# Keys and values of a cross-attention context by seven block products in place of eight

## The chip, the cores and the metric

The kernel runs on one core of a Trainium2 chip. The metric is the device time of one launch in microseconds (us). The engines are called as in the profile: PE (matrix products; PEld is its weight load), DVE (vector), ACT (scalar), POOL (GpSimd) and SP (it only issues DMA transfers here). Each engine takes its instructions strictly in the order in which the program lists them, and waits on semaphores for the others.

## The reference

One transformer block in float32: 16 batch elements of 224 tokens with 512 features, a context of 750 tokens with 512 features for each, 16 heads of 32 features. Biases are left out here:

```python
x_norm = modulate(_ln(x), shift_a, scale_a)            # shift, scale, gate from cond
x = x + gate_a[:, None] * (attention(x_norm) @ W_proj)
q_c  = _ln(x) @ W_qc
kv_c = _ln(context) @ W_kvc                            # (16, 750, 512) @ (512, 1024)
k_c, v_c = jnp.split(kv_c, 2, axis=-1)
x = x + softmax(q_c k_c^T * scale) v_c @ W_cproj       # 16 heads
h = gelu(modulate(_ln(x), shift_m, scale_m) @ W_mlp1) @ W_mlp2
x = x + gate_m[:, None] * h
```

The change touches the lines of `kv_c`, and the residual `x` of the cross attention.

## The kernel before

Three stages follow each other: self attention (to about 728 us), cross attention (about 728 to 2192 us) and the MLP. The change lies in the cross attention, and the MLP already computes its products by blocks in the Winograd form of Strassen's method: seven products of half-sized blocks in place of eight, with sums of blocks made by `combine` and `combine_right`.

**Layout.** A unit is one batch element `b` and one group `g` of four heads (128 features). There are 16 x 4 = 64 units. The context of 750 tokens is six chunks `c` of 125 (`CP`, `CC`), or two halves `hf` of 375 (`HS`). `turn_ctx` transposes a normalised context chunk on PE into PSUM, and ACT copies it into `cxt` (features on partitions). `project_k(b, m, hf)` makes 128 features of the keys for one half by four matmuls of 375 columns, evicted by ACT into `kt`. `project_v(b, c)` makes all 512 features of the values of a chunk by four matmuls of 512 columns, evicted by ACT into `vt`. For each batch element that is 32 matmuls of 375 and 24 of 512. A float32 matmul of the program shows as two records in the trace.

**PSUM.** Eight banks: `ps_s` is one tile of four banks (`sc`, the scores of two context chunks for four heads), `ps_mm` has three banks (`mm`, for projections, transposes and the transposed maxima), `ps_o` one (`o`).

**A unit in three rounds.** `Unit` is a software pipeline over three units: `cur` computes scores, `prev` exponentials, `last` values. The loop is

```python
if last:
    last.values()                       # PE: o <- pt,vt and o <- acc,ones (the "sums")
for n in range(CH):                     # CH = 3
    st = cur.scores(n)                  # PE into sc
    if n == 0 and last:
        last.finish()                   # DVE: reciprocal, product
    cur.keep(n, st)                     # DVE: running maximum "top" (2 ops); ACT: copy pt <- sc
    run(plan, (b, g, 2 * n))            # slot 2n: other work, planned by hand
    if n < 2 and prev:
        prev.subtract(n)                # PE: o <- mc; DVE: pt <- pt,o (3 ops)
    if n == 0 and prev:
        prev.weights(0)                 # ACT: 3 exponentials; POOL: 5 sums "acc"
    run(plan, (b, g, 2 * n + 1))        # slot 2n+1
    if n == 1 and prev:
        prev.weights(1)
cur.maxima()                            # PE transposes of top; DVE: mc
```

The table `plan` holds the other work by (batch element, unit, slot), filled by `at_slot`: six slots in each unit. In it lie the projections of keys and queries for the next unit, the values and transposes of the next batch element, the layer norms (`Norm`: statistics on DVE, the rest on POOL), the loads, and `project` (the attention's output product with the residual) of the batch element before. In `project` DVE adds the bias to the product (`upd<-mm,bcproj`), POOL adds that to `x`, and a store to `x_cross` follows when both chunks of 112 tokens are done. `Ordered` keeps every engine in the order of the calls, so the slot decides the place on every queue.

Of the kernel before, what the change touches and what calls it, by code (L numbers as in the profile page):

```python
# [37 lines left out]
def kernel(  # L38
# [112 lines left out]
    def load_x(pool, src, bufs):  # L151
        t = pool.tile([TP, TC, H], F32, name="x", bufs=bufs)
        nc.sync.dma_start(out=t, in_=src)
        return t
# [232 lines left out]
    def run(plan, key):  # L387
        for f in plan.pop(key, ()):
            f()
# [371 lines left out]
    def gelu(ps, h, m):  # L761
        nc.scalar.activation(h, ps, AF.Gelu_apprx_tanh, bias=bcol[:, o_mlp + m : o_mlp + m + 1])

    class First:


# [62 lines left out]


    wqc, wcproj, wkc, wvc = cw["qc"], cw["proj"], cw["k"], cw["v"]
    cxt_pool = context_pools.enter_context(tc.tile_pool(name="cxt", bufs=3, side="right", reuse_waits="tile"))
    with tc.tile_pool(name="ca", bufs=2, reuse_waits="tile") as ca:
        xs = {}
        xns = {}
        cxt = {}
        xt = {}
        qt = {}
        kt = {}
        vt = {}  # L840
        at = {}
        norms = {}

        def turn_ctx(b, c):
            if c % CH == 0:
                cxt[b, c // CH] = cxt_pool.tile([P, KC, HS], F32, name="cxt")
            ps = ps_mm.tile([P, 512], F32, name="mm")
            for k in range(KC):
                turn(ps[:, k * CP : (k + 1) * CP], cx[b, c][:, k * P : (k + 1) * P], ident[:CP, :CP])
            lo = (c % CH) * CP  # L850
            nc.scalar.copy(
                cxt[b, c // CH][:, :, lo : lo + CP], ps[:, : KC * CP].rearrange("p (k t) -> p k t", k=KC)
            )

        def project_k(b, m, hf):
            if hf == 0:
                kt[b, m] = ca.tile([P, S], F32, name="kt", bufs=2)
            ps = ps_mm.tile([P, 512], F32, name="mm")
            for k in range(KC):
                mm(  # L860
                    ps[:, :HS], wkc[:, k, m * P : (m + 1) * P], cxt[b, hf][:, k, :],
                    start=(k == 0), stop=(k == KC - 1),
                )
            nc.scalar.activation(
                kt[b, m][:, hf * HS : (hf + 1) * HS], ps[:, :HS], AF.Identity,
                bias=bcol[:, o_kvc + m : o_kvc + m + 1],
            )

        def project_v(b, c):
            vt[b, c] = ca.tile([CP, H], F32, name="vt", bufs=2 * CC)  # L870
            ps = ps_mm.tile([P, 512], F32, name="mm")
            lo = (c % CH) * CP
            for k in range(KC):
                mm(
                    ps[:CP, :H], cxt[b, c // CH][:, k, lo : lo + CP], wvc[:, k, :],
                    start=(k == 0), stop=(k == KC - 1),
                )
            nc.scalar.copy(vt[b, c], ps[:CP, :H])

        def fetch(b):  # L880
            xs[b] = load_x(ca, x_self[b], 3)

        def norm_begin(b):
            xns[b] = ca.tile([TP, TC, H], F32, name="xn", bufs=1)
            norms[b] = Norm(
                [xns[b][:, c, :] for c in range(TC)], [xs[b][:, c, :] for c in range(TC)], TP
            )

        def turn_x(b, k):
            if k == 0:  # L890
# [19 lines left out]

        def project(b, c, ps=None):
            if ps is None:
                ps = ps_mm.tile([P, 512], F32, name="mm")
            whole(project_heads(ps, at[b], wcproj, c * TP))
            add_to_x(ca, ps[:TP, :H], xs[b][:, c, :], bcproj[0], None)
            if c == TC - 1:
                lo = b % GB * N
                nc.sync.dma_start(
                    out=x_cross[b // GB][lo : lo + N, :].rearrange("(c p) d -> p c d", p=TP), in_=xs[b]
                )  # L920

        bcproj = []

# [5 lines left out]
        def at_slot(b, g, slot, f):  # L929
            plan.setdefault((b, g, slot), []).append(f)  # L930

        for b in range(B):
            n = b + 1
            for g in range(KC):
                f, m = (b, g + 1) if g < KC - 1 else (n, 0)
                if f < B:
                    for hf in range(2):
                        at_slot(b, g, hf, lambda f=f, m=m, hf=hf: project_k(f, m, hf))
                    at_slot(b, g, (5, 3, 5, 5)[g], lambda f=f, m=m: project_q(f, m))
            if b:  # L940
                at_slot(b, 1, 4, lambda b=b: project(b - 1, 0))
                at_slot(b, 3, 4, lambda b=b: project(b - 1, 1))
            else:
                for c in range(4):
                    at_slot(0, c // 2, 3 + c % 2, lambda c=c: project_v(0, c))
                at_slot(0, 2, 0, make_bcproj)
            at_slot(b, 0, 2, lambda b=b: project_v(b, 4))
            at_slot(b, 0, 4, lambda b=b: project_v(b, 5))
            if n < B:

                for c in range(CH):
                    at_slot(b, 0, 3 if b else 5, lambda n=n, c=c: turn_ctx(n, c))
                    at_slot(b, 2, 3, lambda n=n, c=c: turn_ctx(n, CH + c))
                for c, (u, slot) in enumerate(((1, 2), (2, 2), (2, 4), (3, 3))):
                    at_slot(b, u, slot, lambda n=n, c=c: project_v(n, c))
                for k in range(0, KC, 2):
                    at_slot(b, 3, 2, lambda n=n, k=k: turn_x(n, k))
                at_slot(b, 0, 0, lambda n=n: fetch(n))
                at_slot(b, 1, 1, lambda n=n: norm_begin(n))
                at_slot(b, 1, 1, lambda n=n: norms[n].stats(0))  # L960
                at_slot(b, 1, 3, lambda n=n: norms[n].stats(1))
                at_slot(b, 2, 0, lambda n=n: norms[n].apply())
            if n == B:


                for c in range(4):
                    at_slot(b, 0, 1 + c, lambda c=c: mlp_load(c))
                    at_slot(b, 1, 1 + c, lambda c=c: mlp_norm(c))
                at_slot(b, 2, 2, mlp_begin)
                at_slot(b, 3, 1, lambda: mlp_weights(cw["pool"], "wqc"))  # L970
                for c, (u, slot) in enumerate(((2, 4), (2, 5), (3, 1), (3, 2))):
                    at_slot(b, u, slot, lambda c=c: mlp_turn(ps_mm, c))
            if b + 2 < B:
                for hf in range(2):
                    at_slot(b, 2 * hf, 3 if b or hf else 5, lambda b=b, hf=hf: load_ctx(b + 2, hf))
                    for c in range(CH):
                        at_slot(
                            b, 1 + 2 * hf, (4, 5, 5)[c] - hf, lambda b=b, hf=hf, c=c: cnorms[b + 2, hf].stats(c)
                        )
                    at_slot(b + hf, 3 - 3 * hf, 0, lambda b=b, hf=hf: cnorms[b + 2, hf].apply())  # L980
        for hf in range(2):
            for c in range(CH):
                at_slot(0, hf, 1 + hf + c // 2, lambda hf=hf, c=c: cnorms[1, hf].stats(c))
            at_slot(0, hf, 2 + hf, lambda hf=hf: cnorms[1, hf].apply())

        class Unit:

# [108 lines left out]
            def finish(self):  # L1096
                t = ca.tile([P, N], F32, name="at", bufs=2 * KC)
                normalize(ca, self.o, t)
                at.setdefault(self.b, []).append(t)

        fetch(0)
        for hf in range(2):
            for c in range(hf * CH, (hf + 1) * CH):
                turn_ctx(0, c)
            load_ctx(1, hf)
            project_k(0, 0, hf)
        for k in range(0, KC, 2):
            turn_x(0, k)
        project_q(0, 0)

        units = [(b, g) for b in range(B) for g in range(KC)]
        cur = prev = last = None
        for b, g in units:
            cur, prev, last = Unit(b, g), cur, prev
            if last:
                last.values()
            for n in range(CH):
                st = cur.scores(n)
                if n == 0 and last:
                    last.finish()  # L1120
                cur.keep(n, st)
                run(plan, (b, g, 2 * n))
                if n < 2 and prev:
                    prev.subtract(n)
                if n == 0 and prev:
                    prev.weights(0)
                run(plan, (b, g, 2 * n + 1))
                if n == 1 and prev:
                    prev.weights(1)
            cur.maxima()  # L1130
# [212 lines left out]
```

## Time and profile before

| | |
|---|---|
| median of three runs | 2908.67 us (2907.1 to 2912.02) |
| profiled execution: its span | 2906.1 us; no other time is known of it |
| PE busy | 2834.6 us, 98% |
| DVE, ACT, POOL busy | 1926.2, 1119.7, 1201.5 us |
| granted TensorE clock, mean | 0.993 |
| keys, `mm<-cxt,wkvc` of 375 | 1024 records, 355.0 us |
| values, `mm<-wkvc,cxt` of 512 | 768 records, 354.4 us |
| one batch element in the steady part of the cross attention | 90 us |

The profiled execution's time is its span, from its first instruction to its last. It lies 2.6 us below the median of the runs. "Busy" is time in which an engine had an instruction; a small share of the span is no measure of whether that engine makes others wait. Times of instructions are from the start of the span. In a timeline, the bracket behind a row tells how long the engine stood idle before it, and which work ended that.

### The profile page before, as it was taken

The numbers are of one execution on the slowest core, as the hardware profiler recorded it, in microseconds if no ns is written. First come the engines' busy times: TensorE is split into PE (matmuls) and PEld (weight loads), VectorE is DVE, ScalarE is ACT, GpSimd is POOL, SyncE is SP. The second block draws the span as 40 slices with busy tenths as digits, with TensorE's granted clock in tenths as the row PEclk, the third lists the DMA queues.
The fourth block names the chain that finished last, engine by engine and source line by source line (L and its number), as shares of the span: only waits on it lengthen the run. The fifth ranks groups of instructions, "written<-read, shape, count | busy, mean of one in ns | idle before, by whom it ended". The sixth has DMA issues, their size and how long they took to land. (4 is left out here: it accounts for less than half of the span.)

```text
span 2906.1 us, 47040 instructions
## 1 busy us (share of the span) xinstructions
PE 2834.6 (98%) x19733; PEld 1810.3 (62%) x19733; DVE 1926.2 (66%) x2764; ACT 1119.7 (39%) x1402; POOL 1201.5 (41%) x1357
## 2 busy tenths in 40 slices
PE   8999999998999999999999999999979999999999
PEld 3444444444555565555656556556546888888888
DVE  4666776676478778787787787877775643444343
ACT  1222222221356655665566556655643112112211
POOL 1022222122356666676666766666551210221021
PEclk9999999998999999999999999999999999999999
DMA  5111110100100010100101100000013111110110
GB/s 191 59 33 33 32 33 10 60 11 24 57 32 24 23 35 24 35 26 21 35 24 35 35 19 28 27 33 24 22 44 107 55 37 37 44 58 29 45 44 30
DMA packets 55384, 114.43 MB, mean 39 GB/s; under 512 B 4308, under 2 KB 4372, under 8 KB 55172
## 3 DMA queue, kind: packets, MB, share of 16 engines
q1 hardware_dynamic: 54560, 110.58, 11.8%
q8 instruction: 155, 2.54, 0.4%
q10 hardware_dynamic: 612, 0.85, 0.1%
q14 instruction: 57, 0.47, 0.1%
HBM read 89.33 MB, written 22.09 MB: 38 GB/s over the span
## 5 line engine op out<-in xcount | busy, mean ns | idle before, releaser
L28 POOL TENSOR_TENSOR acc<-acc,pt 125x448 f32<-125x448 f32 x504 | 573.6, 1138 | 39.5
L28 ACT COPY pt<-sc 125x1792 f32<-125x1792 f32 x192 | 317.3, 1653 | 563.1 <-DVE top L28 510.1
L28 DVE TENSOR_TENSOR pt<-pt,o 125x896 f32<-125x896 f32 x384 | 394.2, 1081 | 88.1 <-PE o L28 85.5
L28 DVE TENSOR_TENSOR top<-top,sc 125x896 f32<-125x896 f32 x320 | 346.4, 1083 | 35.4 <-PE sc L28 28.7
L28 PE MATMUL mm<-wkvc,cxt 128*125 128x512 f32 x768 | 354.4, 604 | 6.9 <-ACT kt L28 6.9
L28 PE MATMUL mm<-cxt,wkvc 128*128 128x375 f32 x1024 | 355.0, 489 | 2.3 <-ACT cxt L28 2.3
L28 ACT ACTIVATE pt<-pt 125x896 f32<-125x896 f32 x384 | 338.4, 951 | 20.0 <-DVE pt L28 19.4
L28 POOL TENSOR_TENSOR upd<-upd,gate 112x512 f32<-112x512 f32 (+1 forms) x60 | 79.2, 1321 | 632.9 <-DVE upd L28 628.4
L28 POOL TENSOR_TENSOR acc<-pt 125x448 f32<-125x448 f32 x126 | 143.8, 1141 | 447.7 <-ACT pt L28 447.7
L28 PEld LDWEIGHTS mm<-cxt,wkvc 128*128 128x128 f32 x1024 | 185.6, 191 | 119.8 <-issue 16.6
L28 DVE RECIPROCAL at<-o 128x224 f32<-128x224 f32 x128 | 198.6, 1552 | 72.9 <-PE o L28 72.9
L28 PEld LDWEIGHTS mm<-wkvc,cxt 128*125 128x125 f32 x768 | 136.5, 187 | 171.5 <-issue 153.2
L28 ACT ACTIVATE pt<-sc 112x1792 f32<-112x1792 f32 x64 | 106.5, 1663 | 333.8 <-PE sc L28 333.8
L28 POOL TENSOR_TENSOR rstd<-mv,eps 112x2 f32<-112x2 f32 (+3 forms) x93 | 18.0, 193 | 508.8 <-DVE mv L28 508.8
L28 PE MATMUL sc<-qt,kt 32*125 32x224 f32 x3072 | 201.6, 377 | 14.0 <-ACT pt L28 13.4
L28 PE MATMUL mm<-xt,wqkv 128*128 128x448 f32 x512 | 208.6, 550 | 5.7 <-DVE xt L28 4.7
L28 DVE TENSOR_REDUCE m<-sc 112x8 f32<-112x1792 f32 x64 | 129.6, 2025 | 121.8 <-PE sc L28 121.8
L28 PEld LDWEIGHTS sc<-qt,kt 32*125 32x125 f32 x3072 | 133.1, 183 | 94.1 <-issue 33.8
L28 PE MATMUL o<-pt,vt 125*32 125x224 f32 x3072 | 158.6, 354 | 0.0
L28 PEld LDWEIGHTS mm<-xt,wqkv 128*128 128x128 f32 x512 | 92.0, 190 | 87.6 <-issue 80.4
L28 DVE TENSOR_REDUCE mc<-mm 112x8 f32<-112x512 f32 (+1 forms) x128 | 79.8, 665 | 98.3 <-PE mm L28 98.3
L28 ACT COPY mx<-a 128x512 f32<-128x512 f32 x26 | 15.2, 586 | 327.0 <-POOL upd L28 307.9
(185 smaller groups left out, 4656.5 us busy)
## 6 DMA issues: line engine op xcount, KB each, us to landing
cx<-in_ctx_dram SPq DMA_DIRECT2D x96, 250.0 KB
x<-in_x_dram SPq DMA_DIRECT2D x16, 448.0 KB
x_self<-x SPq DMA_DIRECT2D x16, 448.0 KB
x<-x_self SPq DMA_DIRECT2D x16, 448.0 KB
x_cross<-x SPq DMA_DIRECT2D x16, 448.0 KB
mx<-x_cross SPq DMA_DIRECT2D x28, 256.0 KB
w<-in_L_xcond_W_mlp_dram SPq DMA_DIRECT2D x7, 1024.0 KB
xr<-x_cross SPq DMA_DIRECT2D x28, 256.0 KB
```

The source lines that it names most:

```text
L28: return lambda *args, **kw: self.tc.keep_in_program_order(f(*args, **kw))
```

## The change

Keys and values are computed by blocks. For the keys the two halves of W's columns, the two halves of the features and the two halves of the context's tokens make 2 x 2 blocks. `kv_sums` makes the three sums of blocks of the weights once on DVE (four operations each for keys and values); `ctx_sums` makes the sums of blocks of each context on POOL (four operations of 128 x 750). `project_k(b, r)` makes 128 features of each of two groups `r` and `r + 2`, for all 750 tokens, by seven products of two matmuls of 375 columns; `project_v(b, c)` makes chunks `c` and `c + 3` by seven products of two matmuls of 256 columns. The products run by a generator, `seven`, in four steps that the plan lays in four slots. Two products stay in PSUM and are added to:

```python
def seven(product, bank, keep, add):      # keep: ACT evicts; add: DVE adds PSUM to what was kept
    a = bank()
    product(a, 1, True)
    keep((0, 0), a)
    c = bank()
    product(c, 2, True)
    add((0, 0), c)
    yield
    product(a, 6, False)
    keep((0, 1), a)
    yield
    b = bank()
    product(b, 5, True)
    keep((1, 1), b)
    product(a, 7, False)
    add((1, 1), a)
    yield
    product(b, 3, False)
    add((0, 1), b)
    product(a, 4, False)
    keep((1, 0), a)
```

For each batch element that is 28 matmuls of 375 and 42 of 256. Four products of seven are evicted by ACT and three added by DVE. The plan is laid anew (`u` is the unit's place; the groups come in the order 0, 2, 1, 3):

```diff
+            steps(b, ((0, 0), (0, 1), (0, 3), (0, 4)), lambda b=b: project_k(b, 1))
+            steps(b, ((1, 0), (1, 1), (1, 1), (1, 2)), lambda b=b: project_v(b, 1))
+            steps(b, ((1, 2), (1, 3), (1, 3), (1, 4)), lambda b=b: project_v(b, 2))
             if b:
-                at_slot(b, 1, 4, lambda b=b: project(b - 1, 0))
-                at_slot(b, 3, 4, lambda b=b: project(b - 1, 1))
+                for c in range(TC):
+                    at_slot(b, 0, 1 + c, lambda b=b, c=c: fetch_rest(b - 1, c))
+                    at_slot(b, 1, 1 + 2 * c, lambda b=b, c=c: bias_rest(b - 1, c))
+                    at_slot(b, 2, 1 + 2 * c, lambda b=b, c=c: project(b - 1, c))
...
-                for c in range(CH):
-                    at_slot(b, 0, 3 if b else 5, lambda n=n, c=c: turn_ctx(n, c))
-                    at_slot(b, 2, 3, lambda n=n, c=c: turn_ctx(n, CH + c))
...
+                for c in range(CC):
+                    at_slot(b, 2, c // CH * 2, lambda n=n, c=c: turn_ctx(n, c))
+                at_slot(b, 2, 2, lambda n=n: ctx_sums(n))
+                for k in range(0, KC, 2):
+                    at_slot(b, 2, 4, lambda n=n, k=k: turn_x(n, k))
+                steps(b, ((3, 0), (3, 1), (3, 2), (3, 3)), lambda n=n: project_k(n, 0))
+                steps(b, ((3, 3), (3, 4), (3, 4), (3, 5)), lambda n=n: project_v(n, 0))
...
+                    at_slot(b, 2, 3, lambda b=b, hf=hf: load_ctx(b + 2, hf))
...
+                            b + hf, 3 - 3 * hf, 1 + c, lambda b=b, hf=hf, c=c: cnorms[b + 2, hf].stats(c)
```

So all six transposes of a context, its sums, and both chunks of `project` fall into the third unit of a batch element (before: transposes and `project` each in two units).

The residual is no longer kept from its load to `project`: `fetch` normalises the loaded tile in place, and `fetch_rest` loads each chunk of 112 tokens again later. POOL adds the bias to it (`bias_rest`), DVE adds the product, and each chunk is stored by itself:

```diff
-            add_to_x(ca, ps[:TP, :H], xs[b][:, c, :], bcproj[0], None)
-            if c == TC - 1:
-                lo = b % GB * N
-                nc.sync.dma_start(
-                    out=x_cross[b // GB][lo : lo + N, :].rearrange("(c p) d -> p c d", p=TP), in_=xs[b]
-                )
+            t = xr.pop((b, c))
+            nc.vector.tensor_tensor(t, ps[:TP, :H], t, ALU.add)
+            lo = b % GB * N + c * TP
+            nc.sync.dma_start(out=x_cross[b // GB][lo : lo + TP, :], in_=t)
```

More of the change, by code (lines that the diff above doesn't have):

```diff
@@ L762, in gelu @@
         nc.scalar.activation(h, ps, AF.Gelu_apprx_tanh, bias=bcol[:, o_mlp + m : o_mlp + m + 1])
+    def seven(product, bank, keep, add):
[5 more added lines that the diff above has]
+        add((0, 0), c)
+        yield
+        product(a, 6, False)
+        keep((0, 1), a)
+        yield
+        b = bank()
[3 more added lines that the diff above has]
+        add((1, 1), a)
+        yield
+        product(b, 3, False)
+        add((0, 1), b)
+        product(a, 4, False)
+        keep((1, 0), a)
     class First:
@@ L831, with kv_sums @@
     wqc, wcproj, wkc, wvc = cw["qc"], cw["proj"], cw["k"], cw["v"]
-    cxt_pool = context_pools.enter_context(tc.tile_pool(name="cxt", bufs=3, side="right", reuse_waits="tile"))
+    cxt_pool = context_pools.enter_context(tc.tile_pool(name="cxt", bufs=2, side="right", reuse_waits="tile"))
+    lo2, hi2 = slice(0, 2), slice(2, 4)
+    wlo, whi = slice(0, HT), slice(HT, H)
+    def kv_sums(w, name):
+        ws = cxt_pool.tile([P, 3, 2, HT], F32, name=name, bufs=1)
+        every(combine(
+            nc.vector, w[:, lo2, wlo], w[:, hi2, wlo], w[:, lo2, whi], w[:, hi2, whi],
+            ws[:, 0], ws[:, 1], w[:, lo2, whi], ws[:, 2],
+        ))
+        return {
+            1: w[:, lo2, wlo], 2: w[:, hi2, wlo], 3: ws[:, 2], 4: w[:, hi2, whi],
+            5: ws[:, 0], 6: ws[:, 1], 7: w[:, lo2, whi],
+        }
     with tc.tile_pool(name="ca", bufs=2, reuse_waits="tile") as ca:
-        xs = {}
+        xr = {}
         xns = {}
         cxt = {}
+        cxb = {}
         xt = {}
@@ L842, with mm_bank @@
         norms = {}
+        kv_blocks = []
+        order = (0, 2, 1, 3)
+        def mm_bank():
+            return ps_mm.tile([P, 512], F32, name="mm")
         def turn_ctx(b, c):
@@ L846, in turn_ctx @@
                 cxt[b, c // CH] = cxt_pool.tile([P, KC, HS], F32, name="cxt")
-            ps = ps_mm.tile([P, 512], F32, name="mm")
+            ps = mm_bank()
             for k in range(KC):
@@ L853, in turn_ctx @@
             )
[L855 to L862, printed above, removed]
-                )
[L864 to L867, printed above, removed]
@@ L869, in project_v @@
-        def project_v(b, c):
[L870 to L878, printed above, removed]
-        def fetch(b):
-            xs[b] = load_x(ca, x_self[b], 3)
@@ L883, in norm_begin, with ctx_sums @@
[L883 to L887, printed above, removed]
+        def ctx_sums(b):
+            x0, x1 = cxt[b, 0], cxt[b, 1]
+            tt = cxt_pool.tile([P, 3, 2, HS], F32, name="ctt", bufs=1)
+            every(combine_right(
+                nc.gpsimd, x0[:, lo2], x1[:, lo2], x0[:, hi2], x1[:, hi2],
+                tt[:, 0], tt[:, 1], x1[:, lo2], tt[:, 2],
+            ))
+            cxb[b] = {
+                1: x0[:, lo2], 2: x0[:, hi2], 3: x1[:, hi2], 4: tt[:, 2],
+                5: tt[:, 0], 6: tt[:, 1], 7: x1[:, lo2],
+            }
@@ new lines, in project_k, with product, place, keep @@
+        def project_k(b, r):
+            for i in range(2):
+                kt[b, r + 2 * i] = ca.tile([P, S], F32, name="kt", bufs=4)
+            def product(ps, p, begin):
+                for k in range(2):
+                    mm(
+                        ps[:, :HS], kv_blocks[0][p][:, k, r * P : (r + 1) * P], cxb[b][p][:, k, :],
+                        start=(begin and k == 0), stop=(k == 1), skip_group_check=True,
+                    )
+            def place(at):
+                return kt[b, r + 2 * at[0]][:, at[1] * HS : (at[1] + 1) * HS]
+            def keep(at, ps):
+                m = o_kvc + r + 2 * at[0]
+                nc.scalar.activation(place(at), ps[:, :HS], AF.Identity, bias=bcol[:, m : m + 1])
+            def add(at, ps):
+                nc.vector.tensor_tensor(place(at), ps[:, :HS], place(at), ALU.add)
+            return seven(product, mm_bank, keep, add)
@@ new lines, in project_v, with product, place, keep @@
+        def project_v(b, c):
+            for i in range(2):
+                vt[b, c + CH * i] = ca.tile([CP, H], F32, name="vt", bufs=10)
+            def product(ps, p, begin):
+                for k in range(2):
+                    mm(
+                        ps[:CP, :HT], cxb[b][p][:, k, c * CP : (c + 1) * CP], kv_blocks[1][p][:, k, :],
+                        start=(begin and k == 0), stop=(k == 1), skip_group_check=True,
+                    )
+            def place(at):
+                return vt[b, c + CH * at[1]][:, at[0] * HT : (at[0] + 1) * HT]
+            def keep(at, ps):
+                nc.scalar.copy(place(at), ps[:CP, :HT])
+            def add(at, ps):
+                nc.vector.tensor_tensor(place(at), ps[:CP, :HT], place(at), ALU.add)
+            return seven(product, mm_bank, keep, add)
@@ new lines, in fetch, with fetch_rest, bias_rest @@
+        def fetch(b):
+            xns[b] = t = ca.tile([TP, TC, H], F32, name="xn", bufs=1)
+            nc.sync.dma_start(out=t, in_=x_self[b])
+            ts = [t[:, c, :] for c in range(TC)]
+            norms[b] = Norm(ts, ts, TP)
+        def fetch_rest(b, c):
+            xr[b, c] = t = ca.tile([TP, H], F32, name="xr", bufs=3)
+            nc.sync.dma_start(out=t, in_=x_self[b][:, c, :])
+        def bias_rest(b, c):
+            nc.gpsimd.tensor_tensor(xr[b, c], xr[b, c], bcproj[0], ALU.add)
@@ L912, in project @@
             if ps is None:
-                ps = ps_mm.tile([P, 512], F32, name="mm")
+                ps = mm_bank()
             whole(project_heads(ps, at[b], wcproj, c * TP))
-            add_to_x(ca, ps[:TP, :H], xs[b][:, c, :], bcproj[0], None)
-            if c == TC - 1:
-                lo = b % GB * N
-                nc.sync.dma_start(
-                    out=x_cross[b // GB][lo : lo + N, :].rearrange("(c p) d -> p c d", p=TP), in_=xs[b]
-                )
+            t = xr.pop((b, c))
+            nc.vector.tensor_tensor(t, ps[:TP, :H], t, ALU.add)
+            lo = b % GB * N + c * TP
+            nc.sync.dma_start(out=x_cross[b // GB][lo : lo + TP, :], in_=t)
         bcproj = []
@@ L930, in at_slot, with steps, step @@
             plan.setdefault((b, g, slot), []).append(f)
+        def steps(key, at, job):
+            held = []
+            def step():
+                if not held:
+                    held.append(job())
+                next(held[0], None)
+            for u, slot in at:
+                at_slot(key, u, slot, step)
         for b in range(B):
             n = b + 1
-            for g in range(KC):
-                f, m = (b, g + 1) if g < KC - 1 else (n, 0)
+            for u in range(KC):
+                f, m = (b, order[u + 1]) if u < KC - 1 else (n, 0)
@@ L936 @@
                 if f < B:
-                    for hf in range(2):
-                        at_slot(b, g, hf, lambda f=f, m=m, hf=hf: project_k(f, m, hf))
-                    at_slot(b, g, (5, 3, 5, 5)[g], lambda f=f, m=m: project_q(f, m))
+                    at_slot(b, u, (2, 5, 5, 5)[u], lambda f=f, m=m: project_q(f, m))
+            steps(b, ((0, 0), (0, 1), (0, 3), (0, 4)), lambda b=b: project_k(b, 1))
+            steps(b, ((1, 0), (1, 1), (1, 1), (1, 2)), lambda b=b: project_v(b, 1))
+            steps(b, ((1, 2), (1, 3), (1, 3), (1, 4)), lambda b=b: project_v(b, 2))
@@ L940 @@
             if b:
-                at_slot(b, 1, 4, lambda b=b: project(b - 1, 0))
-                at_slot(b, 3, 4, lambda b=b: project(b - 1, 1))
-            else:
[L944 to L948, printed above, removed]
-            if n < B:
-                for c in range(CH):
-                    at_slot(b, 0, 3 if b else 5, lambda n=n, c=c: turn_ctx(n, c))
-                    at_slot(b, 2, 3, lambda n=n, c=c: turn_ctx(n, CH + c))
[L954 to L957, printed above, removed]
+                for c in range(TC):
+                    at_slot(b, 0, 1 + c, lambda b=b, c=c: fetch_rest(b - 1, c))
+                    at_slot(b, 1, 1 + 2 * c, lambda b=b, c=c: bias_rest(b - 1, c))
+                    at_slot(b, 2, 1 + 2 * c, lambda b=b, c=c: project(b - 1, c))
+            else:
+                at_slot(0, 2, 1, make_bcproj)
@@ L958 @@
+            if n < B:
                 at_slot(b, 0, 0, lambda n=n: fetch(n))
-                at_slot(b, 1, 1, lambda n=n: norm_begin(n))
                 at_slot(b, 1, 1, lambda n=n: norms[n].stats(0))
@@ L972 @@
                     at_slot(b, u, slot, lambda c=c: mlp_turn(ps_mm, c))
+                for c in range(TC):
+                    at_slot(b, 2, 4 + c, lambda b=b, c=c: fetch_rest(b, c))
+                    at_slot(b, 3, 1 + c, lambda b=b, c=c: bias_rest(b, c))
             if b + 2 < B:
                 for hf in range(2):
-                    at_slot(b, 2 * hf, 3 if b or hf else 5, lambda b=b, hf=hf: load_ctx(b + 2, hf))
+                    at_slot(b, 2, 3, lambda b=b, hf=hf: load_ctx(b + 2, hf))
                     for c in range(CH):
                         at_slot(
-                            b, 1 + 2 * hf, (4, 5, 5)[c] - hf, lambda b=b, hf=hf, c=c: cnorms[b + 2, hf].stats(c)
+                            b + hf, 3 - 3 * hf, 1 + c, lambda b=b, hf=hf, c=c: cnorms[b + 2, hf].stats(c)
                         )
-                    at_slot(b + hf, 3 - 3 * hf, 0, lambda b=b, hf=hf: cnorms[b + 2, hf].apply())
+                    at_slot(b + 1, hf, 0, lambda b=b, hf=hf: cnorms[b + 2, hf].apply())
         for hf in range(2):
             for c in range(CH):
-                at_slot(0, hf, 1 + hf + c // 2, lambda hf=hf, c=c: cnorms[1, hf].stats(c))
-            at_slot(0, hf, 2 + hf, lambda hf=hf: cnorms[1, hf].apply())
+                at_slot(0, hf, 1 + c, lambda hf=hf, c=c: cnorms[1, hf].stats(c))
+            at_slot(0, hf, 4, lambda hf=hf: cnorms[1, hf].apply())
         class Unit:
@@ L1098, in finish @@
                 normalize(ca, self.o, t)
-                at.setdefault(self.b, []).append(t)
-        fetch(0)
+                at.setdefault(self.b, {})[self.g] = t
         for hf in range(2):
@@ L1105 @@
             load_ctx(1, hf)
-            project_k(0, 0, hf)
+        ctx_sums(0)
+        kv_blocks.append(kv_sums(wkc, "wsk"))
         for k in range(0, KC, 2):
@@ L1109 @@
         project_q(0, 0)
-        units = [(b, g) for b in range(B) for g in range(KC)]
+        kv_blocks.append(kv_sums(wvc, "wsv"))
+        whole(project_k(0, 0))
+        whole(project_v(0, 0))
+        units = [(b, u) for b in range(B) for u in range(KC)]
         cur = prev = last = None
-        for b, g in units:
-            cur, prev, last = Unit(b, g), cur, prev
+        for b, u in units:
+            cur, prev, last = Unit(b, order[u]), cur, prev
             if last:
@@ L1121 @@
                 cur.keep(n, st)
-                run(plan, (b, g, 2 * n))
+                run(plan, (b, u, 2 * n))
                 if n < 2 and prev:
@@ L1126 @@
                     prev.weights(0)
-                run(plan, (b, g, 2 * n + 1))
+                run(plan, (b, u, 2 * n + 1))
                 if n == 1 and prev:
```

## The prediction

> **What bounds the kernel now.** The page's busy shares come first, then the windows of one batch element each (before the clock: busy time of PE, PEld, DVE, ACT, POOL).
>
> ```profile
> PE 2834.6 (98%) x19733; PEld 1810.3 (62%) x19733; DVE 1926.2 (66%) x2764; ACT 1119.7 (39%) x1402; POOL 1201.5 (41%) x1357
> ...
> 924.00:1014.00 90.00, 89.29 (x706) 53.79 (x705) 71.59 (x87) 52.86 (x64) 59.48 (x66) 1.00 0.09 29
> 2094.00:2184.00 90.00, 71.15 (x626) 45.22 (x626) 71.39 (x98) 42.83 (x45) 50.54 (x55) 0.91 0.16 53
> ```
>
> PE is the bound: 89.3 of 90 us in the steady part. The last batch element has no keys, values and transposes of a next one to make, and 71 us of PE work, yet its four units took about as long as any (22.6, 25.7, 23.6, 22). So a second chain lies just under PE. The timeline of a unit (its sums end on PE at 911.98) shows it:
>
> ```profile
> 911.91 1.04 PE L28 MATMUL sc<-qt,kt 32*125 32x224 f32 x16
> 912.05 1.56 DVE L28 RECIPROCAL at<-o 128x224 f32<-128x224 f32 x1 [1.40 <-PE o L28]
> 912.88 2.79 PE L28 MATMUL mm<-cxt,wkvc 128*128 128x375 f32 x8
> 913.95 1.08 DVE L28 COPY top<-sc 125x896 f32<-125x896 f32 x1
> 915.06 1.09 DVE L28 TENSOR_TENSOR top<-top,sc 125x896 f32<-125x896 f32 x1
> 915.93 2.71 PE L28 MATMUL mm<-cxt,wkvc 128*128 128x375 f32 x8
> 916.20 3.08 DVE L28 TENSOR_TENSOR pt<-pt,o 125x896 f32<-125x896 f32 x3
> 916.26 1.65 ACT L28 COPY pt<-sc 125x1792 f32<-125x1792 f32 x1 [7.38 <-DVE top L28]
> 917.81 0.58 ACT L28 ACTIVATE kt<-mm,bcol 128x375 f32<-128x375 f32 x1
> ```
>
> After the sums DVE needs 4.2 us (reciprocal, product, two of `top`), then ACT copies `pt` for 1.65, and only then does ACT evict a projection: 6.5 us after the sums. PE does not feel it, since each projection takes another bank and 5.3 us of them stand there.
>
> The last batch element also shows POOL late: three norm chains stood before the second group of `acc`, and PE stood 4.94 us before the sums. After it the scores took 1.87 in place of 1.04, at half clock.
>
> ```profile
> 2145.42 0.96 PE L28 MATMUL o<-acc,ones 125*32 125x224 f32 x4 [4.94 <-POOL acc L28]
> 2146.32 1.87 PE L28 MATMUL sc<-qt,kt 32*125 32x224 f32 x16
> ```
>
> **What it removes.** Start to start, eight records of 375 take 2.63 us (889.99 to 892.62), sixteen of 512 take 7.06 (749.48 to 756.54), sixteen of 256 in the MLP's groups 3.46. Keys go from 64 to 56 records, 8 x 0.329 = 2.6 us; values from 48 of 512 (21.2) to 84 of 256 (18.2), 3.0. That is 5.6 us for a batch element, about 90 in all.
>
> **What it adds on the engines.** DVE: six adds of 128x375 (between 0.42 for 256 and 0.69 for 512 columns from PSUM: 0.55) and nine of 125x256 (0.42), 7.1 us for a batch element: 71.6 + 7.1 = 78.7, still under PE. POOL: four of 128x750. The nearest rows are 1.14 for 448 columns, 1.27 to 1.37 for 512; along the slope of the first two 1.76, in proportion to the last 2.0; I take 1.85, so 7.4 us. ACT: as many evictions of keys, twelve of 256 in place of six of 512 (about 0.45 against 0.59). By busy time alone PE would still decide. The order on the queues says otherwise.
>
> **What it moves: the built order, unit by unit.** Bank `a` carries four products, and each waits for the eviction of the one before: product 6 for `keep` of 1, product 7 for `keep` of 6, 4 for DVE's `add` of 7. These evictions stand on ACT behind the `pt` copy and the exponentials, which wait for DVE, which now itself waits for ACT's `keep` before its adds. I walk each unit along its chain, from the end of its sums, with rows of before; statistics are 0.86, a round of two `top` 2.17, three `pt<-pt,o` 3.08, an exponential 0.88.
>
> *Unit 0 (keys).* ACT evicts product 1 at 6.5. PE has only 2.6 us of products 1 and 2 and stands from 3.9 to 6.5. DVE, idle from 4.2, adds (7.1), subtracts (10.2), statistics, `top` (13.2), statistics, subtracts (17.1), statistics, adds (18.5), `top` (20.7), adds (21.2). The maxima need that bank: 0.7, then values 2.35 and sums 0.4: **24.7**. PE work in it is only 18.
>
> *Unit 1 (two values).* `keep` 1 at 6.35, add (6.8), subtract (9.9), exponentials on ACT (10.8), `keep` 6 (11.25), product 7 (12.3), add, statistics, `top` (15.8), ACT's copy (17.4), two evictions (18.4), add, subtract (21.9), add, statistics, `top` (25.3), copy (27.0), the last eviction (27.5), whose bank the maxima need; 28.1, values, sums: **30.9**.
>
> *Unit 2.* Three `cxt` copies stand on ACT behind the `pt` copy and hold all three banks, so `project` starts at 6.5 and ends at 10.1; scores (11.0), `top` (13.2), copy (14.9), three more `cxt` (16.7). Then POOL's four block sums (24.2) stand before the second five of `acc` (5.93: 30.2), which PE's sums need: **30.6**. Without POOL the bank waits (`project` again from 15.6 to 19.1, scores, `top`, copy 23.8, `xt`, maxima 25.6) would give 28.4.
>
> *Unit 3 (keys, a value).* As unit 0 to `top` at 13.2; then the copy (14.9) and `keep` 5 (15.5) stand before DVE's add (16.1); statistics, subtract (20.0), two adds (21.0), statistics, `top` (24.1), copy (25.8), `keep` of the value's product 6 (26.2), product 7, query, 3 and 4 (30.3), maxima, values, sums: **33.7**.
>
> Together 119.8 us for 90: 29.8 more. Batch elements 1 to 14 pay that: 417. Element 0 has no earlier unit at its start: about 106 for the 102 it takes now, +4. The last has units 0 and 1 dear and the others as now: about 99 for 94, +5. Ahead of the first unit, keys and values of one step each stand with the block sums in place of keys alone: six transposes and copies to 732.2, POOL's third sum at 737.9, then the seven and seven products (12 us) and small waits: first scores at 751.5, not 742.3: +10, between +5 (sums hidden) and +15. DVE's eight weight sums (0.7 to 1.0 us each) lie beside that.
>
> Edits at nothing: the second load of the residual, its smaller stores and the moved context loads go to SP, whose transfers land with long cover (1.5 MB issued at about 20 us of unit 2, first read 10 us into unit 3, some 20 us later, 75 GB/s; a window of the trace moved 362). If that cover were gone, DVE's statistics would hold the round by a few us. `bias_rest` replaces an add of the same size on POOL.
>
> **The clock.** Rows: gaps of 2.69, 3.47 and 4.94 us on PE in the last batch element were each followed by some 3 to 7 us at half clock, one of 2.26 by none. The walk has seven gaps of 2.6 to 3.9 us for a batch element. At about 3 us of half clock each loses 1.5 us of PE work; that lies on the chain in unit 2 (`project`, scores), at the end of unit 3 and partly in unit 1. I take 5 us of 10; bounds 0 and 10: 15 x 5 = 75, from 0 to 150.
>
> The Trainium skill, "TensorE: Matmul & The Clock Gate", Part 1, says that the clock halves after an idle window of about 3.4 us, free-running; by it only the gaps of 3.7 and 3.85 count, some 3 us for a batch element, and the sum would be 30 us lower. The 2.69 row speaks for the larger count.
>
> Sum: 2906.1 + 10 + 4 + 417 + 5 + 75 = 3417 of span, and 2.6 to the median: **3420**.
>
> **Rivals.** (a) *PE remains the bound, faster.* If evictions kept ahead of the bank, 16 x 5.6 less and 10 more give 2830. For it: PE at 98%, all others under 80%. Against: it decides at the first eviction; `keep` 1 would have to be done by 3.9 us after the sums, and the `pt` copy before it ends at 5.9 in every unit. (b) *Only POOL counts*: banks hidden, and the block sums cost one wait before the sums like the 4.94 in each batch element: 90 - 5.6 + 5 = 89.4, and 2909 in all, no change. (c) *Half of the walk*: DVE and ACT make up part of the waits across units, 15 for 30: 2906 + 210 + 20 = 3140, with some clock loss 3150. Against: each unit of the walk starts from its own sums, so little can be carried. That the change doesn't do what it says is excluded: the built order has 28 and 42 matmuls, and four sums on POOL.
>
> **Chances.** Forecast 0.85; (c) 0.10; (a) 0.04; (b) 0.01. The forecast's own range runs from no clock loss and shorter handoffs (3300) to twice the loss and 2.0 us on POOL (3510); to hold 8 in 10 with errors of the walk of 3 us a unit, 3250 to 3540. A difference of 0.2% is about what a measurement of this kernel can tell; faster 0.04, same 0.01, slower 0.95.
>
> **What would show it.** Right: the sums of `o<-acc,ones` stand 25, 31, 31 and 34 us apart; PE waits for ACT `kt`, `vt` and `cxt` (2.6 us and more each) and in the third unit for POOL `acc` behind `ctt` rows of 1.85; PE busy near 80%, mean clock near 0.93. Wrong: units of 22 us or less, no PE waits over 1 us on evictions; or batch elements of 105 us, where engines carry work across units.

## The result and the profile after

The changed kernel takes 3408.26 us (median of four runs, 3404.74 to 3410.16) where the kernel before takes 2910.35 beside it: a ratio of 1.1712, 95% interval 1.1695 to 1.1729. The forecast was 3420 us, with a range of 3250 to 3540.

The page's busy shares of the changed kernel, and the row of its costliest group, ACT's copy of the scores (the number behind the bar is idle time of ACT just before the copies, and what ended it):

```profile
span 3406.7 us, 48595 instructions
...
PE 2926.2 (86%) x20181; PEld 1956.1 (57%) x20181; DVE 2033.6 (60%) x3012; ACT 1141.6 (34%) x1498; POOL 1307.4 (38%) x1421
...
L28 ACT COPY pt<-sc 125x1792 f32<-125x1792 f32 x192 | 317.3, 1652 | 843.6 <-DVE top L28 807.6
```

The same row of the kernel before:

```profile
L28 ACT COPY pt<-sc 125x1792 f32<-125x1792 f32 x192 | 317.3, 1653 | 563.1 <-DVE top L28 510.1
```

No engine is near its limit any more. PE went from 98% to 86% of a longer span, and all the others lost share too. ACT stood 808 us before these copies until DVE's maxima were done, where it had stood 510.

What PE itself waited for, in 900 us of the cross attention (about 7.4 batch elements; us in total, times, longest):

```profile
PE mm L28 <- ACT vt L28: 72.6, 34, 2.9
PE mm L28 <- ACT kt L28: 53.9, 28, 2.6
PE mm L28 <- ACT cxt L28: 44.3, 14, 3.6
PE mm L28 <- ACT xt L28: 15.6, 13, 2.1
PE mm L28 <- DVE kt L28: 7.0, 16, 0.8
```

ACT's four rows are 186 us, 25 for each batch element. Before the change the largest such row, in 1150 us, was half a microsecond for a batch element:

```profile
PE mm L28 <- ACT kt L28: 6.0, 13, 0.5
```

The windows of four units in a row, each from the start of its first scores, right behind the sums, to that of the next (units 1, 2 and 3 of one batch element, then 0 of the next; columns as in the windows before):

```profile
1513.24:1544.92 31.68, 26.39 (x196) 19.53 (x192) 19.51 (x27) 13.06 (x18) 18.97 (x23) 0.84 0.00 1
1544.92:1575.13 30.21, 21.63 (x188) 13.45 (x184) 17.51 (x19) 14.09 (x18) 18.41 (x15) 0.94 0.20 58
1575.13:1609.87 34.74, 26.93 (x196) 18.19 (x192) 20.63 (x29) 14.07 (x18) 15.43 (x18) 0.95 0.12 35
1609.87:1633.88 24.01, 20.57 (x168) 13.05 (x164) 19.37 (x26) 12.55 (x14) 12.68 (x13) 0.93 0.01 2
```

In the mean of batch elements 1 to 14 units 0 to 3 take 24.0, 31.3, 32.3 and 34.7 us, 122.3 together, where the kernel before takes 22.7, 21.3, 22.9 and 22.6, 89.5. The unit 2 shown is one of the two shortest of fourteen: both its output products (`project`) ran at full speed, and the others took 31.9 to 33.5 us.

The timeline of unit 3 (its scores start at 1575.13, as the sums before them end), for comparison with the one shown of before:

```profile
1576.10 2.79 PE L28 MATMUL mm<-cxt,wkvc 128*128 128x375 f32 x8
...
1579.50 1.65 ACT L28 COPY pt<-sc 125x1792 f32<-125x1792 f32 x1 [8.89 <-DVE top L28]
1581.05 0.58 ACT L28 ACTIVATE kt<-mm,bcol 128x375 f32<-128x375 f32 x1
1581.66 0.55 DVE L28 TENSOR_TENSOR kt<-mm,kt 128x375 f32<-128x375 f32 x1 [2.27 <-ACT kt L28]
1581.68 1.53 PE L28 MATMUL mm<-ctt,wsk 128*128 128x375 f32 x4 [2.36 <-ACT kt L28]
1582.12 3.07 DVE L28 TENSOR_TENSOR pt<-pt,o 125x896 f32<-125x896 f32 x3
...
1598.54 1.65 ACT L28 COPY pt<-sc 125x1792 f32<-125x1792 f32 x1 [1.54 <-DVE top L28]
1600.08 0.65 ACT L28 COPY vt<-mm 125x256 f32<-125x256 f32 x2
1600.51 1.83 PE L28 MATMUL mm<-wkvc,cxt 128*125 128x256 f32 x4 [2.64 <-ACT vt L28]
```

Products 1 and 2 of the keys are done by 1578.9, but ACT begins to evict product 1 only at 1581.05, behind the `pt` copy. Both PE (product 6, in the same bank) and DVE (its add) stand until that is done, 2.36 and 2.27 us. The last three lines are the same chain again at the end of the unit: DVE's maxima, ACT's copy, ACT's eviction, and PE's product 7 behind them.

### The profile page after: what moved, and what is told of

It is laid out like the page before. It is cut to its first block, busy times and chain, and to the rows that moved or that the text cites. A ratio compares the mean times of both kernels' runs of the same rounds, so it can differ in the third digit from the quotient of the medians.

```text
span 3406.7 us, 48595 instructions
## 1 busy us (share of the span) xinstructions
PE 2926.2 (86%) x20181; PEld 1956.1 (57%) x20181; DVE 2033.6 (60%) x3012; ACT 1141.6 (34%) x1498; POOL 1307.4 (38%) x1421
## 5 line engine op out<-in xcount | busy, mean ns | idle before, releaser
L28 ACT ACTIVATE pt<-pt 125x896 f32<-125x896 f32 x384 | 348.7, 955 | 94.5 <-DVE pt L28 87.2
L28 DVE TENSOR_TENSOR top<-top,sc 125x896 f32<-125x896 f32 x320 | 345.6, 1080 | 22.7 <-PE sc L28 16.0
L28 PE MATMUL sc<-qt,kt 32*125 32x224 f32 x3072 | 218.1, 401 | 19.5 <-ACT pt L28 19.5
L28 PE MATMUL mm<-wcproj,at 128*112 128x512 f32 x240 | 151.3, 789 | 88.6 <-ACT cxt L28 88.6
L28 PE MATMUL mm<-wkvc,cxt 128*125 128x256 f32 x576 | 160.6, 418 | 77.2 <-ACT vt L28 77.2
L28 PEld LDWEIGHTS sc<-qt,kt 32*125 32x125 f32 x3072 | 143.8, 198 | 116.3 <-issue 83.9
L28 DVE TENSOR_TENSOR vt<-mm,vt 125x256 f32<-125x256 f32 x144 | 60.7, 422 | 225.0 <-PE mm L28 163.8
L28 PEld LDWEIGHTS mm<-wkvc,cxt 128*125 128x125 f32 x576 | 107.7, 197 | 117.7 <-ACT vt L28 91.6
L28 PE MATMUL o<-pt,vt 125*32 125x224 f32 x3072 | 169.7, 372 | 0.0
L28 PE MATMUL mm<-ctt,wsk 128*128 128x375 f32 x256 | 100.6, 517 | 75.3 <-ACT kt L28 71.1
L28 PE MATMUL mm<-cxt,wkvc 128*128 128x375 f32 x384 | 137.2, 492 | 15.7 <-ACT kt L28 15.7
```

The costliest lines, as they stand in the source:

```text
L28: return lambda *args, **kw: self.tc.keep_in_program_order(f(*args, **kw))
```

## The experiments

The theory on trial: what the change costs is the place of the evictions on ACT's queue, behind copies that wait for DVE, with one bank that four products share. Rivals: DVE's and POOL's added work itself; the moves of transposes and output products; POOL's block sums alone.

**e1: eight products again, all else as changed.** The short diff (four `cxt` buffers, no sums of blocks; `project_k` and `project_v` are those of before):

```diff
-            steps(b, ((0, 0), (0, 1), (0, 3), (0, 4)), lambda b=b: project_k(b, 1))
-            steps(b, ((1, 0), (1, 1), (1, 1), (1, 2)), lambda b=b: project_v(b, 1))
-            steps(b, ((1, 2), (1, 3), (1, 3), (1, 4)), lambda b=b: project_v(b, 2))
+            for c, (u, slot) in enumerate(((0, 2), (0, 4), (1, 2), (1, 4)), 2):
+                at_slot(b, u, slot, lambda b=b, c=c: project_v(b, c))
...
+                    for hf in range(2):
+                        at_slot(b, u, hf + (4 if u == 2 else 0), lambda f=f, m=m, hf=hf: project_k(f, m, hf))
```

> The changed kernel with keys and values by eight products again, each in a bank of its own, evicted once by ACT; the transposes in one unit, both output products in that unit and the residual by chunks stay (four cxt buffers; the keys of the last group in slots 4 and 5 of unit 2, so that unit carries 5.3 us more PE work). Theory (evictions that the next product of the same bank waits for stand on ACT behind the pt copy, and DVE behind them): units 0, 1 and 3 go back to about 22 us, unit 2 stays at 31 to 33 through its waits for cxt copies: some 98 for a batch element, about 3040 us in all. Rival A (the moves of transposes and output products cost it, not the block products): over 3250. Rival B (block products alone): about 2910.

Measured: 3186.42 us, ratio 1.0949 (1.0917 to 1.0981); units 22.8, 24.5, 36.8 and 24.0 us, 108.2 together. It lies between the theory (3040) and rival A (over 3250). Unit 2 is dear with plain products too: PE stands for the `cxt` copies as in the changed kernel, and then runs `project` at half clock, here 5.38 us for 3.69:

```profile
1553.25 5.38 PE L28 MATMUL mm<-wcproj,at 128*112 128x512 f32 x8 [3.61 <-ACT cxt L28]
1564.17 5.38 PE L28 MATMUL mm<-wcproj,at 128*112 128x512 f32 x8 [2.72 <-ACT cxt L28]
```

So the layout alone, with the keys that I had put into unit 2, brings 18.7 of the 33 us: rival A holds for unit 2. It is the same mechanism (three banks held until ACT has copied them behind `pt`), but the block products are not its only victims. In units 0, 1 and 3, which have the block products, about 18.6 of the 23.4 us that the change had added went away with them, though e1 also lays the projections differently over the units.

**e2: ACT's copy behind the even slot's work.** `copy` is the second half of `keep`, unchanged:

```diff
                 run(plan, (b, u, 2 * n))
+                cur.copy(st)
```

> The changed kernel with one line moved: ACT's copy pt <- sc is issued behind the work of the even slot, not ahead of it, so that evictions of that slot no longer wait for DVE's maxima. No work is removed. Theory: unit 0 22.4, unit 1 25.4, unit 2 26.5 (POOL's block sums now decide it), unit 3 26, together 100 for 122, about 3100 us in all. Rival (the added DVE and POOL work itself costs it, wherever the evictions stand): within 50 us of 3408.

Measured: 3108.32 us, ratio 1.0681 (1.0650 to 1.0712); units 21.7, 27.0, 26.5 and 27.2 us, 102.4 together, 20 less, with not one instruction removed. The timeline of its unit 0 shows the eviction 2.5 us after the sums, in place of 5.9:

```profile
1574.35 2.79 PE L28 MATMUL mm<-cxt,wkvc 128*128 128x375 f32 x8
...
1575.91 0.57 ACT L28 ACTIVATE kt<-mm,bcol 128x375 f32<-128x375 f32 x1 [5.43 <-PE mm L28]
1576.53 1.09 DVE L28 TENSOR_TENSOR top<-top,sc 125x896 f32<-125x896 f32 x1
...
1577.41 1.44 PE L28 MATMUL mm<-ctt,wsk 128*128 128x375 f32 x4
...
1577.71 1.65 ACT L28 COPY pt<-sc 125x1792 f32<-125x1792 f32 x1 [1.22 <-DVE top L28]
```

PE goes from product 2 to 6 without a gap. That 300 of the 500 us hang on one place in ACT's queue shows the theory for these; the rival that the added work alone costs them falls, for the work is all there. The other 200 are the matter of e5 to e7.

**e3: block sums later.**

```diff
-                at_slot(b, 2, 2, lambda n=n: ctx_sums(n))
+                at_slot(b, 2, 4, lambda n=n: ctx_sums(n))
```

> The changed kernel with POOL's four block sums of the context moved from slot 2 to slot 4 of unit 2, behind the second five of acc. Theory: PE's own chain through the cxt copies lies just under POOL's in that unit, so 1 to 2 us for a batch element: about 3385, 3365 to 3405. Rival (POOL is what makes unit 2 dear): 7 us or more for a batch element, 3300 or less.

Measured: 3404.64 us, ratio 1.1699 (1.1665 to 1.1733). That is 4 us below the changed kernel and at the edge of the range given, and the runs of both overlap; unit 2 takes 32.0 us for 32.3. POOL is not what makes unit 2 dear.

**e4: without DVE's adds.**

```diff
             def add(at, ps):
-                nc.vector.tensor_tensor(place(at), ps[:, :HS], place(at), ALU.add)
+                pass
```

The same line of `project_v` goes too.

> The changed kernel without DVE's nine plus six adds of products to keys and values (those sums are left out, all seven products and the four evictions stay). 7 us of DVE work less for a batch element. Theory (the adds also tie DVE to ACT's evictions): unit 0 3 us less, unit 1 5, unit 3 5 to 6, unit 2 as it is: 14 less for a batch element, about 3200. Rival (only the DVE work counts): 7 less, about 3305. Rival (ACT and PE alone decide it): within 30 us of 3408.

Measured: 3299.31 us, ratio 1.1337 (1.1304 to 1.1370); units 21.4, 28.3, 34.4 and 31.1, 7 less together. A miss for the theory's number. The total is the DVE work of the adds, as the rival said, but by chance. Units 0, 1 and 3 lost 2.6, 3.0 and 3.6 us, 9.1 in all, and their adds are 1.6, 2.5 and 2.9. Unit 2 gained 2.1, although nothing was changed in it. None of its 28 output products ran at full speed, where 6 of 28 did in the changed kernel; a pair took 11.7 us in the mean for 10.3, which is 1.4 of the 2.1. One pair of e4:

```profile
1618.92 5.23 PE L28 MATMUL mm<-wcproj,at 128*112 128x512 f32 x8 [3.89 <-ACT cxt L28]
1629.69 6.67 PE L28 MATMUL mm<-wcproj,at 128*112 128x512 f32 x8 [2.72 <-ACT cxt L28]
```

So the adds cost their length on a chain that has no slack; that they also tie DVE to ACT is worth some 2 us in these three units, and not the 7 that I had reckoned.

**e5: e2 and e3 together.**

> e2 (ACT's copy behind the even slot's work) with the block sums in slot 4 too. In e2 unit 2 measured 26.5 us and PE stood 5.0 us for acc behind the block sums, which in the changed kernel itself (e3) were hidden by the bank waits. Theory (a wait uncovered by the one removed): now the same move is worth 5 us for a batch element, 102.4 to 97, about 3035 us in all. Rival (the block sums cost nothing, as e3 said): 3108 as in e2.

Measured: 3007.80 us, ratio 1.0343 (1.0313 to 1.0373); unit 2 20.6 us, all four 95.4. The same move that brought at most a few us in e3 brings 100 here, since in e2 this wait stands open:

```profile
1545.25 0.96 PE L28 MATMUL o<-acc,ones 125*32 125x224 f32 x4 [5.01 <-POOL acc L28]
```

That is 7 for a batch element and not 5: behind the wait e2's matmuls had run at half clock (the first scores of unit 3 in 1.87 us), and in e5 they do not (1.04).

**e6: e5 with the first exponentials behind the odd slot.**

```diff
-                if n == 0 and prev:
-                    prev.weights(0)
                 run(plan, (b, u, 2 * n + 1))
+                if n == 0 and prev:
+                    prev.weights(0)
```

> e5 with the first three exponentials of a unit issued behind the odd slot's work, so that the eviction of product 6 no longer waits for them (nor for DVE's subtraction). In e2 PE stood 3.8 us for that eviction in unit 1 and 1.1 in unit 3. Theory: unit 1 24, unit 3 26, together 93, about 2975 us in all. Rival (DVE's chain decides already, PE's wait only fills its slack): within 15 us of e5.

Measured: 2928.51 us, ratio 1.0064 (1.0041 to 1.0086); units 21.9, 22.8, 20.6 and 24.8, 90.1 together. PE's wait before product 7 in unit 1, 3.79 us in e5 (first row), is 1.19 in e6 (second):

```profile
1551.54 2.07 PE L28 MATMUL mm<-wkvc,cxt 128*125 128x256 f32 x4 [3.79 <-ACT vt L28]
...
1508.08 1.13 PE L28 MATMUL mm<-wkvc,cxt 128*125 128x256 f32 x4 [1.19 <-ACT vt L28]
```

**e7: e6 with statistics in the last slot.**

```diff
-                            b + hf, 3 - 3 * hf, 1 + c, lambda b=b, hf=hf, c=c: cnorms[b + 2, hf].stats(c)
+                            b + hf, 3 - 3 * hf, (1, 5, 5)[c], lambda b=b, hf=hf, c=c: cnorms[b + 2, hf].stats(c)
```

The two statistics of `x` in unit 1 move to slot 5 as well.

> e6 with two of the three layer-norm statistics of a unit (0.86 us each on DVE) moved to the last slot, where DVE stands while PE makes the maxima and the values. Theory (DVE's chain through a unit is now the bound): 1 to 1.7 us less in units 0, 1 and 3, together about 89, 2920 us in all. Rival (PE decides by then): within 10 us of e6.

Measured: 2903.50 us (eight runs), ratio 0.9978 (0.9967 to 0.9989): faster than before, by 0.2%. Only unit 0 became shorter (20.3); units 1 and 3 stayed at 22.8 and 24.8, where PE's own work is about as long (21.6 and 24.3). So both held, each in its units: DVE's chain in unit 0, PE in the others.

**e8: the residual by chunks alone, on the kernel before.** The diff is that of the change's third part, with `bias_rest` in slot 5 of units 0 and 2.

> The kernel before with the third part of the change alone: the residual loaded again by chunks, the bias added on POOL, stores by chunks; output products stay in units 1 and 3. Theory: no difference, 2905 to 2915. Rival (twice the loads and stores, or the order on SP, hold the norms): over 2930.

Measured: 2914.92 us, ratio 1.0021 (1.0007 to 1.0034). That is within the numbers I gave, but the interval lies above no change. In the profiled run elements 1 to 14 are 6.1 us longer, by unit 2 (23.3 us for 22.9), and the first scores come 4.8 us later. The cause of both stays open.

**e9: three more places.**

```diff
-        ctx_sums(0)
         kv_blocks.append(kv_sums(wkc, "wsk"))
+        ctx_sums(0, nc.vector)
...
-                    at_slot(b, 1, 1 + c, lambda c=c: mlp_norm(c))
+                    at_slot(b, 1, 4 + c // 2, lambda c=c: mlp_norm(c))
...
-                    at_slot(b, u, (2, 5, 5, 5)[u], lambda f=f, m=m: project_q(f, m))
+                    at_slot(b, u, (1, 5, 5, 5)[u], lambda f=f, m=m: project_q(f, m))
```

> e7 with three places mended that its trace shows: the first context's block sums on DVE in place of POOL (PE stood 4.3 us for them ahead of the first unit), the MLP's first norms behind the second five of acc in the last batch element (PE stood 4.8 us there), and the query of unit 0 one slot earlier (PE stood 0.6 us before the second scores). Theory (PE decides again, each wait is worth itself): 5 + 5 + 15 x 0.6 less than e7, about 2885 us, 2880 to 2895. Rival (DVE decides): 2895 to 2903.

Measured: 2903.95 us, ratio 0.9982 (0.9973 to 0.9991), no better than e7. The first scores started 4.2 us sooner and the last element's unit 1 fell from 29.0 to 22.8, but unit 0 rose from 20.3 to 21.0 in every batch element. PE had lost the work that covered ACT's copy before the third scores, and POOL was late for the sums:

```profile
1570.77 1.04 PE L28 MATMUL sc<-qt,kt 32*125 32x224 f32 x16 [1.32 <-ACT pt L28]
...
1578.90 0.57 PE L28 MATMUL o<-acc,ones 125*32 125x224 f32 x4 [0.44 <-POOL acc L28]
```

**e12: e9 with the query back in slot 2.**

> e9 with the query of unit 0 back in slot 2. In e9 the 4.2 us ahead of the first unit and 5 us in the last batch element were won, and unit 0 lost 0.7 us (21.0 for 20.3: PE now stood 1.3 us before the third scores and 0.4 for acc). Theory (the query was work that covered the copy before the third scores): 88.5 us for a batch element as in e7, and e7's time less 9 us, 2890 to 2898. Rival (the loss in unit 0 comes from POOL's later sums): as e9, 2904.

Measured: 2892.48 us, ratio 0.9942 (0.9929 to 0.9956). This version beats both kernels: 0.6% less than before, 15% less than the changed one.

```profile
PE 2768.2 (96%) x20181; PEld 1889.1 (65%) x20181; DVE 2043.0 (71%) x3016; ACT 1138.5 (39%) x1498; POOL 1301.2 (45%) x1417
...
1500.00:1588.00 88.00, 83.98 (x731) 58.31 (x732) 77.13 (x102) 53.12 (x69) 65.53 (x68) 1.00 0.12 34
```

The records are the same 20181 as in the changed kernel. PE is at 84 of 88 us again, the clock at full speed, and unit 0 is back at 20.3 us, so the query was the cover there. Against the trace of before, elements 1 to 14 are 13.6 us shorter, element 0 11.0 and the last 4.0, and the first scores come 11.2 us later. So of the 4.3 us of PE work saved for a batch element (the sum is below) 1.0 reaches the time.

**e10: the moves on ACT of e6 on the kernel before.**

> The kernel before, eight products, with the same two moves on ACT as e6 (copy behind the even slot, first exponentials behind the odd slot). Theory (PE was busy 89.3 of 90 us there and its evictions were waited for by nobody): no difference, 2900 to 2915. Rival (the moves alone made e7 faster than before, not the block products): 2890 or less.

Measured: 2920.85 us, ratio 1.0039 (1.0026 to 1.0053); a batch element takes 89.8 us for 89.5. So these two moves are no gain in themselves; with them and those of e5, e7 and e12 the block products are one. The later moves were not tried on the kernel before. One of them, the MLP's norms behind `acc`, might shorten it too: its last batch element has such a wait (the 4.94 us shown in the prediction).

**e11: e9 with values by eight products.**

> e9 with values by eight products again, six evictions of 512 for each batch element, keys by seven. (The values of chunks 3 to 5 are made from a block that the sums have overwritten; the work is the same.) PE has 2.8 us more for a batch element, DVE 3.8 less, ACT six evictions less. Theory (PE decides): 1.5 to 2.8 us more for a batch element than e9, 25 to 45 us more in all. Rival (DVE's chain and the evictions decide): as e9 or faster.

Measured: 2951.40 us, ratio 1.0146 (1.0132 to 1.0160), 47 us above e9: 92.3 us for 89.2 in a batch element, with unit 1 at 25.1 for 22.8. PE's work decides there, a little beyond the 2.8 us I had given it.

## Why the prediction was right, step by step

**The walk.** Its four units were 24.7, 30.9, 30.6 and 33.7 us; measured 24.0, 31.3, 32.3 and 34.7. The steps inside hold too: ACT's first eviction 5.9 us after the sums in unit 3 (walk 5.9), the `pt` copy of the third round ending at 25.1 (walk 25.8). e2 confirmed them from the other side: walked with the copy moved, 100 us for a batch element and 3100 in all; measured 102 and 3108.

**The prices.** DVE's adds took 0.54 and 0.42 us (0.55, 0.42), POOL's four sums 6.7 (7.4), ACT's evictions of 256 columns 0.38 (0.45). PE's busy work for a batch element fell from 88.8 (89.3 of 90) to 84.5 (86.0 of 90 in e7, where the clock is at full speed), 4.3 and not 5.6; where the rest went stays open.

**Where errors cancelled.** By stages, measured from the first scores, the sums and the spans of the two traces (us more than before):

| | forecast | measured |
|---|---|---|
| ahead of the first scores | 10 | 14.8 (757.14 for 742.30) |
| batch element 0 | 4 | 16.5 |
| elements 1 to 14, with their clock loss | 417 + 70 | 459.8 |
| the last | 5 + 5 | 8.0 |
| behind the last sums | 0 | 1.5 |
| all, span against span | 511 | 500.6 |

Element 0 was mis-sized: it was given 106 us and took 119.3 (18.3, 34.3, 33.7 and 33.0), so only its unit 0 is shorter than the others. Ahead of it the context was ready at 732.8, about as forecast, but POOL began the block sums at 736.1, straight behind residual adds of the self attention that the forecast left out. PE stood 4.2 us for the third sum and then ran eight records of 375 in 5.37 us, twice their time.

The clock term held. PE's busy time is 94.6 us in the mean of elements 1 to 14, for 84.5 of work, so half clock cost it about 10 us, as forecast, of which 5 were put on the chain. Above the walk with unit 2 by PE's own chain (117.6, for which the next paragraph gives the reason) lie 4.7.

**What was wrong in the reasons.** In unit 2 I let POOL's block sums decide (30.6 us), with 28.4 by PE's own chain through the bank waits. In none of the elements 1 to 14 did PE wait for `acc`. In the unit shown (1544.92 to 1575.13) POOL is done at 1574.33, 0.3 us before PE comes to the sums, since the values ran at half clock (3.53 us for 2.48):

```profile
1551.46 3.69 PE L28 MATMUL mm<-wcproj,at 128*112 128x512 f32 x8 [3.61 <-ACT cxt L28]
...
1560.69 3.69 PE L28 MATMUL mm<-wcproj,at 128*112 128x512 f32 x8 [2.72 <-ACT cxt L28]
...
1569.55 4.78 POOL L28 TENSOR_TENSOR acc<-acc,pt 125x448 f32<-125x448 f32 x4
...
1571.30 3.53 PE L28 MATMUL o<-pt,vt 125*32 125x224 f32 x48
1574.65 0.55 PE L28 MATMUL o<-acc,ones 125*32 125x224 f32 x8
```

And with the block sums out of the way the unit still takes 32.0 us (e3). So the 2.2 us that POOL adds to the walk are not there in these elements; half clock filled their place, since the unit took 30.2 us where `project` ran at full speed both times and 32.6 in the mean of the others. That the walk's 30.6 lies near the measured 32.3 is luck in part. It is also most of what the forecast of an element has too much: 119.8 and 5 for the clock, against 122.3. POOL decided only in unit 2 of element 0 (PE stood 4.4 us for `acc`) and where the bank waits were gone (e2). Three of the signs named came differently: no wait for `acc`, PE busy 86% and not near 80%, a mean clock of 0.952 and not near 0.93.

**The rivals.** The kernel before has 5.3 us of projections as cover for the first eviction, and that is enough: moving the copy and the exponentials there brought nothing (e10). (a), PE as the bound, needed `keep` 1 by 3.9 us after the sums. With the copy moved it is there at 3.1 (e2), and with POOL and the exponentials out of the way too, PE is the bound and the kernel gains (e7, e12). So the point of decision was named rightly, and the changed kernel stands on its wrong side. (b) and (c) fell to the unit times.

## What to carry to other kernels

Before one bank is given several products in a row, look at what stands ahead of the eviction on its engine's queue: each product now waits for all of it, where the kernel before, with a bank for each, waited for next to nothing (half a microsecond for a batch element). Walk one round of the pipeline along the built order with durations of the old trace; the walk gave 119.8 us for a batch element of 122.3, in unit 2 partly by luck, though busy shares spoke for a gain. When such a loss is found, move instructions before giving the idea up: here moves alone, with no work removed, turned 17% more into 0.6% less. And try them together, since a wait can hide another: the block sums' move brought at most a few us while the copy stood in its old place, and 100 behind it.

## What the runs showed of the hardware

PE's half clock, at which matmuls take nearly twice their time, does not follow the length of PE's idle gap before it. In elements 1 to 14 of the changed kernel `project` stands behind gaps of 3.61 and 2.72 us, 28 times in all: 6 times it ran at its full speed (3.69 us), 22 times in 5.1 to 6.7. In the four windows shown both ran at full speed, but a gap of 2.34 was followed by scores of 1.87 us for 1.04, one of 2.36 by scores of 1.04, and one of 2.08 by the values of 3.53 for 2.48. The Trainium skill, "TensorE: Matmul & The Clock Gate", Part 1, describes a free-running window of about 3.4 us, which fits that equal gaps end differently. That gaps of 2.1 and 2.3 us can do it does not fit an idle window of that length; here the rows decide.
